# Pairwise field interactions: GpSimd's loads in 8 KB packets, for tiles 4 to 30 instead of 2 to 26

## The chip, the cores and the metric

The kernel runs on one core of one Trainium2 chip. The metric is the device time of one launch in microseconds (us). The kernel before was run six times: median 1326.73 us, lowest 1326.18, highest 1327.6. A smaller time is better.

## What is computed

There are 4096 rows; each has 32 fields of 64 float32 numbers. For each of the 496 pairs of fields (i < j), field i is multiplied by that pair's own 64x64 matrix, and the product is multiplied, element by element, by field j:

```python
i_idx, j_idx = np.triu_indices(32, k=1)
vi = inputs[:, i_idx, :]                       # (4096, 496, 64)
vj = inputs[:, j_idx, :]
vdotw = jnp.einsum('bpd,pde->bpe', vi, W)      # W: (496, 64, 64)
inter = vdotw * vj
return inter.reshape(B, -1)                    # (4096, 31744)
```

The input is 33.6 MB, the matrices 8.4 MB with their padding, and the output 520 MB: the kernel is, before anything else, a writer.

## The kernel before, in words

**Tiles.** The 4096 rows are cut into 32 tiles of 128 rows (row = partition). A tile of x is 128 partitions of 2048 floats, so 8 KB for each partition and 1 MB in all; its output is 128 partitions of 31744 floats, 16.25 MB. All the matrices stay in SBUF in the tile `w`. They come in five pieces on SP's queue (line 194, the list `LOADS`), 928 KB to 2592 KB each.

**Work on one tile.** `transpose_x` (lines 177 to 183) turns x with TensorE, and ScalarE copies the result into `xT`. For each pair p of fields (2p, 2p+1), TensorE multiplies `xT` by the pair's matrices into PSUM (line 222), and VectorE multiplies what is in PSUM by the other fields of x into the SBUF tile `ring` (lines 232 and 240). When the pairs of one of the four groups in `STORES` are done, SP issues that group's store (line 246): 3776, 3264, 3936 and 4896 KB. `ring` has room for 28160 floats a partition, less than one tile's 31744, so VectorE's writes to a part of it wait until the store that last read that part is complete. A store's 128 rows go out on 16 DMA engines, 8 rows on each, every row as one packet of 26112 to 39168 bytes.

**Loads of x.** `xbuf` has three slots of one tile. `x_slots` (line 34) pairs the tiles into loads: tile 0 alone, then (1,2), (4,3), (5,6), (8,7), and so on. The load of tiles t+1 and t+2 stands ahead of tile t's work (lines 200 to 202). A pair none of whose tiles is in `LIGHT_TILES` is one 2 MB DMA from ScalarE's queue (line 157), with 16 KB packets, since the two slots lie side by side. In the other pairs the odd tile is a 1 MB DMA from ScalarE's queue with 8 KB packets, and the even one is issued by GpSimd in `load_beside` (lines 131 to 145). GpSimd's load waits only for its own slot.

**Which DMA engines a GpSimd load uses.** The code assumes a cursor[...]. `from_engine(e)` (lines 119 to 129) moves the cursor to engine e with a tiny DMA, a "nudge" of k rows of 32 bytes. `load_beside` issues four DMAs for a tile:

- a nudge to one of the engines in `PAIRS_FROM`;
- the tail, partitions 120 to 127 (64 KB): 2 engines, 4 rows of 8 KB on each;
- a nudge to engine 5 (`LIGHT + 1`);
- the head, partitions 0 to 119 (960 KB): 15 engines from number 5 round to number 3. Engine `LIGHT` = 4 carries nothing of it. The head is cut into left and right halves of the rows, so that each of the 15 engines gets 16 pieces of 4 KB.

`HEAD` is 120 and `REST` is 4 here. The host lays x out in the order in which the DMAs read it (lines 261 to 276), with 16 floats of padding behind each of the tail's two blocks. GpSimd issues these 52 DMAs in program order and nothing else of weight. Its tiles are 2, 4, ... 26, thirteen of 32.

Of the kernel before, what the change touches and what calls it, by code (L numbers as in the profile page):

```python
# [12 lines left out]
P = 128  # L13
# [10 lines left out]

DMA_ENGINES = 16
LIGHT = 4
LIGHT_TILES = range(2, 28, 2)
PAIRS_FROM = [6, 8, 10, 12, 14, 0, 1]
HEAD = P - P % (DMA_ENGINES - 1)
REST = (P - HEAD) // 2  # L30
PAD = 16


def x_slots(NT):


    loads = [[(0, 0)]]
    for t in range(1, NT, 2):
        if t + 1 == NT:
            loads.append([(t, 1)])  # L40
        elif loads[-1][-1] == (t - 1, 2):
            loads.append([(t + 1, 0), (t, 1)])
        else:
            loads.append([(t, 1), (t + 1, 2)])
    return loads
# [3 lines left out]
def pair_bilinear_kernel(  # L49
# [33 lines left out]
    NT = out.shape[1] * 2 // (F * (F - 1) * D)  # L83
# [16 lines left out]
    def runs(tl, a, b, n):  # L100
# [3 lines left out]

    xbuf = const.tile([P, 3 * F * D], F32, tag="x", name="x")
    x_loads = x_slots(NT)
    x_sizes = [
        sum(P * F * D + (2 * PAD if t in LIGHT_TILES else 0) for t, s in load) for load in x_loads
    ]
    slot = {t: xbuf[:, ts(s, F * D)] for load in x_loads for t, s in load}  # L110

    nudges = [const.tile([DMA_ENGINES, 16], F32, tag=f"nudge{i}", name=f"nudge{i}") for i in range(2)]
    cursor = 0

    def from_pool(out, in_):

        tc.keep_in_program_order(nc.gpsimd.dma_start(out=out, in_=in_))  # L117

    def from_engine(e):

        nonlocal cursor
        k = (e - cursor) % DMA_ENGINES
        if k:
            nudge = nudges[e == LIGHT + 1]
            from_pool(
                nudge[:k].rearrange("p (h c) -> p h c", h=2)[:, :, :4],
                x[: k * 8].rearrange("(p h c) -> p h c", p=k, h=2),
            )
        cursor = e

    def load_beside(at, xt, lap):

        nonlocal cursor
        n = F * D
        from_engine(PAIRS_FROM[lap % len(PAIRS_FROM)])
        g = REST * n + PAD
        tail = x[at + HEAD * n : at + HEAD * n + 2 * g].rearrange("(g c) -> g c", g=2)
        from_pool(xt[HEAD:], tail[:, : REST * n])
        cursor += 2
        from_engine(LIGHT + 1)  # L140
        from_pool(
            xt[:HEAD].rearrange("p (h c) -> p h c", h=2),
            x[at : at + HEAD * n].rearrange("(h p c) -> p h c", h=2, p=HEAD),
        )
        cursor = LIGHT

    def load_x(load):

        at = sum(x_sizes[: x_loads.index(load)])
        parts = [[(t, s)] for t, s in load] if any(t in LIGHT_TILES for t, s in load) else [load]  # L150
        for part in parts:
            t, s = part[0]
            n = len(part) * F * D
            if t in LIGHT_TILES:
                load_beside(at, slot[t], LIGHT_TILES.index(t))
            else:
                nc.scalar.dma_start(
                    out=xbuf[:, s * F * D : s * F * D + n],
                    in_=x[at : at + P * n].rearrange("(p c) -> p c", p=P),
                )  # L160
            at += P * n + (2 * PAD if t in LIGHT_TILES else 0)

    pring = psum.tile([P, BANKS * BANK], F32, tag="pring", name="pring")
    bank = 0
# [21 lines left out]
    at = 0  # L186

    load_x(x_loads[0])
    w_sb = const.tile([P, sum(width[0::2])], F32, tag="w", name="w")
    done = 0  # L190
# [7 lines left out]
    for t in range(NT):  # L198
        xt = slot[t]
        for load in x_loads:  # L200
            if min(load)[0] == t + 1:
                load_x(load)
        for s, group in enumerate(STORES):
            if at + store_w[s] > RING:
                at = 0
# [3 lines left out]
            for p in group:  # L209
# [5 lines left out]
                for c1 in range(first, width[2 * p] + 1, BANK):  # L215
                    n = first if c1 == first else BANK
# [78 lines left out]
```

## Time and profile before

| | before |
|---|---|
| median of six runs | 1326.73 us |
| the profiled execution | 1326.36 us |
| its span, first to last instruction | 1324.2 us |
| mean granted TensorE clock | 0.967 |
| TensorE busy | 1161.5 us (88%) |
| VectorE busy | 1183.2 us (89%) |
| ScalarE busy | 66.1 us (5%) |
| GpSimd busy | 32.5 us (2%) |
| moved by DMA | 562.9 MB, 425 GB/s over the span |

Times on the page are microseconds unless marked ns. The page cuts the span into 40 slices; a digit is the busy share in tenths. A DMA packet is what one DMA engine moves at one go for one queue. The queues are q1 (SP: stores and w), q10 (ScalarE: x), q0 (GpSimd: x and nudges) and two that fetch instructions (q8 and q14). The trace keeps start, duration, queue and size of every packet, but not the number of the DMA engine that moved it.

### The profile page before, as it was taken

Reading aid. Unit: us, or ns where it says so; the run is one execution under the profiler, and the core shown is the slowest. Engines: PE = TensorE matmul, PEld = TensorE weight load, DVE = VectorE, ACT = ScalarE, POOL = GpSimd, SP = SyncE. Lnnn points to the kernel's source line nnn. Section 1 sums busy time; section 2 is a strip of 40 time slices with the busy share of each in tenths; the row PEclk is TensorE's granted clock in tenths of the full one; section 3 lists DMA queues with packets and bytes.
Section 4 is the critical chain, followed back from the end, with each engine's and each line's share of the span. In section 5 each row is a group of like instructions: output and inputs, shape, how many; then the busy total and the mean of one; then the engine's idle time right before and its main releaser. Section 6 shows DMA issues by size and latency. Waiting matters only on the chain.

```text
span 1324.2 us, 13175 instructions
## 1 busy us (share of the span) xinstructions
PE 1161.5 (88%) x5376; PEld 541.1 (41%) x5376; DVE 1183.2 (89%) x1376; ACT 66.1 (5%) x65; POOL 32.5 (2%) x58
## 2 busy tenths in 40 slices
PE   5998989989898998998889889898998979989893
PEld 3443444434343434444344444334444434443441
DVE  4898989989899998998899899898998989989894
ACT  0000000000000000000000000000000000000000
POOL 1000000000000000000000000000000000000000
PEclk9999999999999998999999989999998989989997
DMA  9999999999999999999999999999999999999998
GB/s 336 434 427 433 426 433 430 431 429 425 430 431 429 432 430 428 430 431 433 424 429 426 429 431 426 430 427 434 427 425 432 431 426 434 423 429 432 427 424 358
DMA packets 27068, 562.90 MB, mean 425 GB/s; under 512 B 4584, under 2 KB 4584, under 8 KB 7960
## 3 DMA queue, kind: packets, MB, share of 16 engines
q1 hardware_dynamic: 19152, 528.49, 93.3%
q10 hardware_dynamic: 2448, 19.92, 3.6%
q0 software_dynamic: 5408, 13.65, 2.7%
q8 instruction: 42, 0.69, 0.2%
q14 instruction: 18, 0.15, 0.0%
HBM read 41.95 MB, written 520.09 MB: 424 GB/s over the span
## 4 chain that ended last, share of the span: by engine, by line
DMA 48%; DVE 37%; issue 8%; PE 4%; DVEq 0%; ACT 0%
DMA out_dram<-ring 48%; DVE ring L232 32%; DVE ring L240 5%; PE pring L222 4%; DMA x<-in_x_dram 1%; PE pring L182 0%; DVEq L232 0%; ACT xT L183 0%; DVEq L291 0%; DVEq L240 0%
## 5 line engine op out<-in xcount | busy, mean ns | idle before, releaser
L222 PE MATMUL pring<-w,xT 64*128 64x512 f32 (+4 forms) x4864 | 1097.0, 561 | 133.4 <-DVE ring L232 113.2
L232 DVE TENSOR_TENSOR ring<-pring,x 128x1024 f32<-128x1024 f32 (+3 forms) x1056 | 1104.3, 1107 | 113.2 <-DMA out_dram<-ring 81.2
L222 PEld LDWEIGHTS pring<-w,xT 64*128 64x128 f32 x4864 | 484.1, 190 | 704.4 <-DVE ring L232 524.2
L183 ACT COPY xT<-pring 128x1024 f32<-128x1024 f32 x64 | 64.8, 1012 | 1213.1 <-PE pring L182 1213.1
L240 DVE TENSOR_TENSOR ring<-pring,x 128x64 f32<-128x64 f32 (+3 forms) x320 | 97.5, 355 | 10.0 <-DMA out_dram<-ring 8.9
L182 PEld LDWEIGHTS pring<-ident,x 128*128 128x128 f32 x512 | 57.0, 144 | 59.0 <-DVE ring L232 47.9
L182 PE MATMUL pring<-ident,x 128*128 128x128 f32 x512 | 72.5, 286 | 9.7 <-DMA x<-in_x_dram 9.6
L117 POOL DMA_DIRECT2D x<-in_x_dram x26 | 17.2, 663 | 911.0 <-DVE ring L240 911.0
L117 POOL DMA_DIRECT2D nudge<-in_x_dram x26 | 14.7, 567 | 4.4 <-DMA nudge<-in_x_dram 4.2
L183 ACT ACT_TABLE_LOAD x1 | 1.3, 1283 | 1.7 <-PEq L287 1.7
masks.py:199 POOL TENSOR_SCALAR_AFFINE_SELECT ident<-ident 128x128 f32<-128x128 f32 x1 | 0.3, 287 | 0.1
masks.py:197 POOL MEMSET ident<- 128x128 f32 x1 | 0.2, 205 | 0.3 <-POOLq L287 0.3
L287 POOL MEMSET const-float32-0.0<- 128x1 f32 x1 | 0.1, 93 | 0.2 <-issue 0.2
L287 POOL MEMSET const-bfloat16-1.0<- 128x1 bf16 x1 | 0.1, 95 | 0.0
L287 POOL MEMSET const-uint8-127<- 128x1 uint8 x1 | 0.1, 95 | 0.0
L287 POOL MEMSET const-float32-1.0<- 128x1 f32 x1 | 0.1, 93 | 0.0
## 6 DMA issues: line engine op xcount, KB each, us to landing
out_dram<-ring SPq DMA_DIRECT2D x32, 4896.0 KB, 17.7
out_dram<-ring SPq DMA_DIRECT2D x32, 3936.0 KB, 17.7
out_dram<-ring SPq DMA_DIRECT2D x32, 3776.0 KB, 18.6
out_dram<-ring SPq DMA_DIRECT2D x32, 3264.0 KB, 19.9
x<-in_x_dram ACTq DMA_DIRECT2D x15, 1024.0 KB, 18.9
x<-in_x_dram POOLq DMA_DIRECT2D x13, 960.0 KB, 33.7
x<-in_x_dram ACTq DMA_DIRECT2D x2, 2048.0 KB, 21.6
w<-in_w_dram SPq DMA_DIRECT2D x1, 2592.0 KB, 33.8
```

The costliest lines, as they stand in the source:

```text
L117: tc.keep_in_program_order(nc.gpsimd.dma_start(out=out, in_=in_))
L182: nc.tensor.transpose(pt[:, ts(c, P)], xt[:, ts(n * g + c, P)], ident)
L183: nc.scalar.copy(xT[:, ts(g, 2 * BANK)], pt)
L222: nc.tensor.matmul(pm[:, h * BANK : h * BANK + n], xT[h * D : (h + 1) * D, ts(p, P)], w_sb[h * D : (h + 1) * D, a : a + n], start=True, st ...
L232: nc.vector.tensor_tensor(runs(osb, o[0], o[1], n), runs(pm, 0, BANK, n), bass.AP(xj.tensor, xj.offset, [xj.ap[0], [0, 2], xj.ap[1]]), ALU ...
L240: nc.vector.tensor_tensor(osb[:, o[h] + h * D : o[h] + n], pm[:, h * (BANK + D) : h * BANK + n], xj[:, h * D :], ALU.mult,)
L287: nc = bacc.Bacc("TRN2", target_bir_lowering=False, num_devices=1)
```

## The change

The tiles that GpSimd loads become 4 to 30, even numbers without 16: again thirteen. Tiles 2 and 16 are now in pairs that hold no tile of GpSimd, (1,2) and (16,15), so each of these pairs is one 2 MB DMA on ScalarE's queue. Tiles 28 and 30 leave the 2 MB DMAs of before, and 27 and 29 come as 1 MB DMAs from ScalarE.

In `load_beside` the head is no longer cut into half rows. Both parts are now blocks of whole rows with 16 floats of padding behind each block: 2 blocks of 4 rows for the tail, 15 blocks of 8 rows for the head. The order (nudge, tail, nudge, head), the engines meant and the list `PAIRS_FROM` stay.

```diff
-LIGHT_TILES = range(2, 28, 2)
+LIGHT_TILES = [4, 6, 8, 10, 12, 14, 18, 20, 22, 24, 26, 28, 30]
 PAIRS_FROM = [6, 8, 10, 12, 14, 0, 1]
-HEAD = P - P % (DMA_ENGINES - 1)
-REST = (P - HEAD) // 2
+HEAD = P // DMA_ENGINES
+REST = HEAD // 2
 PAD = 16
...
-        n = F * D
-        from_engine(PAIRS_FROM[lap % len(PAIRS_FROM)])
-        g = REST * n + PAD
-        tail = x[at + HEAD * n : at + HEAD * n + 2 * g].rearrange("(g c) -> g c", g=2)
-        from_pool(xt[HEAD:], tail[:, : REST * n])
-        cursor += 2
-        from_engine(LIGHT + 1)
-        from_pool(
-            xt[:HEAD].rearrange("p (h c) -> p h c", h=2),
-            x[at : at + HEAD * n].rearrange("(h p c) -> p h c", h=2, p=HEAD),
-        )
-        cursor = LIGHT
+        most = DMA_ENGINES - 1
+        for e, k, rows, p in (
+            (PAIRS_FROM[lap % len(PAIRS_FROM)], 2, REST, most * HEAD),
+            (LIGHT + 1, most, HEAD, 0),
+        ):
+            from_engine(e)
+            n = rows * F * D
+            blocks = x[at : at + k * (n + PAD)].rearrange("(k c) -> k c", k=k)
+            from_pool(xt[p : p + k * rows], blocks[:, :n])
+            at += k * (n + PAD)
+            cursor = (e + k) % DMA_ENGINES
```

The rest of the diff gives x the new sizes and lays it out on the host to match.

More of the change, by code (lines that the diff above doesn't have):

```diff
@@ L106, in pair_bilinear_kernel @@
     x_loads = x_slots(NT)
-    x_sizes = [
-        sum(P * F * D + (2 * PAD if t in LIGHT_TILES else 0) for t, s in load) for load in x_loads
-    ]
+    pads = (DMA_ENGINES + 1) * PAD
+    tile_sizes = [P * F * D + (pads if t in LIGHT_TILES else 0) for t in range(NT)]
+    x_sizes = [sum(tile_sizes[t] for t, s in load) for load in x_loads]
     slot = {t: xbuf[:, ts(s, F * D)] for load in x_loads for t, s in load}
@@ L160, in load_x @@
                 )
-            at += P * n + (2 * PAD if t in LIGHT_TILES else 0)
+            at += sum(tile_sizes[t] for t, s in part)
     pring = psum.tile([P, BANKS * BANK], F32, tag="pring", name="pring")
@@ L269 @@
             if t in LIGHT_TILES:
-                x.append(rows[:HEAD, t].reshape(HEAD, 2, -1).transpose(1, 0, 2).ravel())
-                tail = np.zeros((2, REST * F * D + PAD), rows.dtype)
-                tail[:, : REST * F * D] = rows[HEAD:, t].reshape(2, -1)
-                x.append(tail.ravel())
+                k = (DMA_ENGINES - 1) * HEAD
+                for part in (
+                    rows[k:, t].reshape(2, REST * F * D),
+                    rows[:k, t].reshape(DMA_ENGINES - 1, HEAD * F * D),
+                ):
+                    x.append(np.pad(part, ((0, 0), (0, PAD))).ravel())
             else:
```

## The prediction

> **What bounds the kernel now.** I read the 40 slices first, then busy time by stage, the DMA queues, the DMA issues, and last the packets themselves.
>
> ```profile
> DVE  4898989989899998998899899898998989989894
> ...
> DMA  9999999999999999999999999999999999999998
> GB/s 336 434 427 433 426 433 430 431 429 425 430 431 429 432 430 428 430 431 433 424 429 426 429 431 426 430 427 434 427 425 432 431 426 434 423 429 432 427 424 358
> ```
>
> The DMA engines are full in every slice; VectorE, the next, has gaps throughout. So the end is set by the bytes and by the pace of the 16 DMA engines. Two slices are below some 425 GB/s: the first and the last. By stage:
>
> ```profile
> 2.00:8.00 6.00, 0.00 (x0) 0.00 (x0) 0.00 (x0) 0.95 (x1) 2.13 (x4) 1.00 0.93 371
> 8.00:27.00 19.00, 12.87 (x54) 6.80 (x56) 10.30 (x10) 1.01 (x1) 0.60 (x1) 1.00 1.03 326
> 27.00:34.00 7.00, 7.00 (x40) 5.07 (x38) 6.58 (x8) 1.01 (x1) 0.00 (x0) 1.00 0.99 424
> ...
> 60.00:1300.00 1240.00, 1114.62 (x5166) 516.08 (x5163) 1137.37 (x1320) 61.73 (x61) 26.75 (x45) 0.97 1.00 429
> 1300.00:1324.20 24.20, 3.67 (x22) 1.84 (x19) 6.30 (x12) 0.00 (x0) 0.00 (x0) 0.63 0.76 328
> ```
>
> The last two numbers of a line are DMA share and GB/s. From 8 to 27 us the engines are fully busy and yet move only 326 GB/s: packets take longer there. In the last stretch they are 76% busy: some engines have finished while others run on. These two are what the change can touch.
>
> ```profile
> q1 hardware_dynamic: 19152, 528.49, 93.3%
> q10 hardware_dynamic: 2448, 19.92, 3.6%
> q0 software_dynamic: 5408, 13.65, 2.7%
> ...
> x<-in_x_dram ACTq DMA_DIRECT2D x15, 1024.0 KB, 18.9
> x<-in_x_dram POOLq DMA_DIRECT2D x13, 960.0 KB, 33.7
> x<-in_x_dram ACTq DMA_DIRECT2D x2, 2048.0 KB, 21.6
> ```
>
> q0 takes 0.198% of the engines' time per MB (2.7/13.65), q10 0.181%.
>
> **The packets.** On one engine a packet starts 3 to 4 ns before the one ahead of it ends, so the records can be joined into 16 chains, one for each engine (identities can swap where two engines coincide). Four readings:
>
> - Usual durations: 159 ns for 4096 bytes, 309 for 8192, 611 for 16384; a store's row 968 (26112 bytes) to 1448 (39168).
> - In the slow stage a w packet of 7424 bytes takes 370 ns (281 alone), 13312 bytes 706 (some 497 at the rate of the rest), 16128 bytes 758 (601 alone), x of 8192 bytes 410, x of 4096 bytes 205. The excess of all loads after 8.1 us is 79.4 us, 4.96 us an engine. It begins with w's second piece beside tile 1 (q10), goes on beside tile 2 (q0), and is gone within a microsecond of tile 2's last packet at 26.7: w alone runs at 601 and 771 ns (20736 bytes). The stores' first rows start at 34.4 us on the median engine, 32.4 on the first.
> - One engine is slow throughout: 33 ns more than usual on the median store row from 980 us on; its excess is 8.5 us there, the others' 0.4 to 2.8. It is the one that carries none of GpSimd's heads. Until tile 26's head (959 to 980 us) it stays within about 1.5 us of the median engine; from 1003 to 1306 us it falls from 1.27 ahead to 4.60 behind, 0.8 us a tile. It ends at 1322.70, the next at 1321.96, the median at 1318.9.
> - During a head the slow engine gets 16 empty packets of 4 bytes in place of 16 pieces. In seven heads its packets took 1.10 to 2.27 us over the usual, of which 22 x 33 ns = 0.73 is its own slowness: 23 to 96 ns an empty packet, mean 62.
>
> [...] 15 chains get pieces, one gets none. [...] GpSimd's head, 16 packets an engine, lands after 33.7 us, ScalarE's load, 8 packets, after 18.9. [...] here 2 x 159 - 309 = 9 ns. [...]
>
> **The change part by part.**
>
> *8 KB packets.* 120 pairs of 4 KB become 120 packets of 8 KB in 13 tiles: 120 x 13 x 9 ns = 14.0 us, over 15 engines 0.9 us each. It lies on the bound. The tails keep their form. Loads land sooner, which nobody waits for.
>
> *Empty packets.* Tails of 4 rows give 4 empty packets on each other engine (728 = 13 x 14 x 4 in q0's count), so a head of 8 rows should give 8 instead of 16. Of the 12 later heads, 96 empty packets fewer: 96 x 62 ns = 6.0 us on the slow engine; ends 2.2 and 9.2. Nothing excludes that one costs more when it is rarer; I take zero as the outer bound.
>
> *Which tiles.* The slow engine is spared thirteen heads before and after. Tiles 28 and 30 spare it at about 1040 and 1120 us, where it falls behind now; tile 2's relief (2.0 us in the first store's start) and tile 16's are lost. Its total stays; only the empty packets make it shorter. Because it has no gaps of its own, its end moves with its total.
>
> *The start.* Tile 2 leaves q0. Up to 7.3 us (w's first piece and tile 0 at usual durations) nothing changes. Then 8 rounds of 281 ns (w) and 611 ns (tiles 1 and 2) make 7.14 us. The unknown is whether they slow each other. Below: not at all, as w's first piece beside tile 0. Above: w stays slow for all of its middle pieces. I take the ratio of w beside tile 1, 370/281 and 410/309, 1.33: 9.5 us, to 16.8. Then w alone: 8 x 497 = 4.0, 8 x 601 = 4.8, 8 x 771 = 6.2: 31.8 us in place of 34.4, **2.6 us** saved. VectorE covers this: the first store is issued at 23.93 us, long before; tile 0's last store is issued at 57.87 while the engines have rows until 61.95, 4 us of cover. Without the slowing, 29.4 us, 5.0 saved, and perhaps 0.3 lost because that cover is used up. The slow engine carries tile 2 now and is 2% slower: 32.4, no gain there.
>
> *What is moved past whom.* On ScalarE one DMA replaces a tile's; it is 5% busy. Tiles 15 and 16 wait for the later slot and land in 21.6 us instead of 18.9; tile 1's start at 57.75 and the turning of tile 2 at 85.44 show 27.7 us until the data is needed, so 6 us of cover remain. If that were gone, TensorE would wait once. On GpSimd the first tail, tile 4's, waits for tile 0's end as now:
>
> ```profile
> 8.31 0.60 POOL L117 DMA_DIRECT2D nudge<-in_x_dram  x1 [4.17 <-DMA nudge<-in_x_dram]
> 58.14 0.57 POOL L117 DMA_DIRECT2D x<-in_x_dram  x1 [49.23 <-DVE ring L240]
> ```
>
> Behind it are only its own loads, needed tens of us later. SP's queue is untouched.
>
> *Sum.* Slow engine: 1322.70 - 6.0 = 1316.7. The next engine: 1321.96 - 2.6 - 0.9 = 1318.5, which is then last. That is 4.2 us before 1322.70. The profiled execution took 1326.36 (span 1324.2 and 2.2 around it), so 1322.1; the median of the runs is 0.4 higher: **1322.5**.
>
> **Rivals.**
>
> *No slowing left at the start* (25%). For it: w's first piece and tile 0 are both at usual durations, and most of the slow stage has q0 in it. Against: w and tile 1 slow each other from 8.2 us, three before q0's first 4 KB piece at 11.24. 5.0 - 0.3 in place of 2.6: 1320.4.
>
> *The slow engine stays last* (17%). Empty packets cost the same whatever their number, or are still 16. Its total is then as before: 1322.7 less 2.2 to 0, so 1324.5 to 1326.7.
>
> *Slower* (7%). w's middle pieces stay slow to the end although tile 2 has left q0, and the slow engine has tile 2 on top: 7.3 + 1.35 x 1.02 x (2.25 + 4.9 + 4.0 + 4.8) + 6.3 = 35.6 us in place of 32.4. With no help from empty packets: +3.2, 1329.9. It decides from where the slow engine's first store row starts later than 32.4 by more than the empty packets give back.
>
> *The change doesn't do what it says* (3%). [...] The tails, of the same form, go to two engines today.
>
> **Numbers.** Likeliest 48%, 1322.5 (own range 1321 to 1324.3). The range 1319.8 to 1326.3 leaves out the slower cases and the edges. About 0.2%, 2.65 us, is what a measurement can tell from no change, so faster is under 1324.1: the likeliest case, the first rival and a little of the second, 0.75; same 0.16; slower 0.09.
>
> **What would show it.** Right: no 4096-byte packets in q0; the stage from 8 to 27 us well above 326 GB/s, first store rows near 31.8; 104 empty head packets in place of 208; the slow engine no longer last. Wrong: w still at 700 ns after tile 2's last packet, or one engine still 3 us behind the median at the end.

## The result and the profile after

The kernel after takes 1322.74 us (median of 18 runs, 1320.04 to 1325.33); the kernel before, run again beside it, 1326.41 (38 runs). The ratio is 0.9971, 95% interval 0.9965 to 0.9977: 3.7 us or 0.3% faster, where 1322.5 had been forecast. The profiled execution of the kernel after took 1323.68 us, with a span of 1321.5.

First the same two rows of slices, and q0, of the kernel after:

```profile
DMA  9999999999999999999999999999999999999998
GB/s 392 434 429 431 429 427 426 434 433 420 427 428 412 440 421 429 430 429 431 428 429 428 430 434 424 430 425 426 423 433 426 425 428 424 424 431 430 428 434 377
...
q0 software_dynamic: 3744, 13.65, 2.5%
```

The first slice rose from 336 to 392 GB/s and the last from 358 to 377; in between some slices are lower than before (412, 420, 421). q0 moves the same 13.65 MB in 3744 packets instead of 5408: 1560 fewer x packets, and 104 fewer empty ones, as counted ahead. By stage:

```profile
2.00:8.00 6.00, 0.00 (x0) 0.00 (x0) 0.00 (x0) 0.94 (x1) 0.27 (x1) 1.00 0.95 381
8.00:27.00 19.00, 16.71 (x68) 8.21 (x70) 12.08 (x12) 2.02 (x2) 0.00 (x0) 1.00 1.01 430
27.00:34.00 7.00, 7.00 (x36) 2.92 (x32) 7.00 (x8) 0.00 (x0) 0.00 (x0) 1.00 1.03 412
...
60.00:1300.00 1240.00, 1113.78 (x5152) 516.36 (x5154) 1135.78 (x1318) 61.74 (x61) 26.50 (x47) 0.98 1.00 428
1300.00:1321.50 21.50, 2.09 (x14) 0.98 (x10) 4.05 (x10) 0.00 (x0) 0.00 (x0) 0.59 0.81 350
```

From 8 to 27 us the engines now move 430 GB/s, not 326: the slow stage is gone entirely, not in part. The long middle is a little slower, 428 in place of 429 (428.02 and 429.22 before rounding), which over 1240 us is some 3 us. The loads of GpSimd do land sooner (26.3 us in place of 33.7), and nobody was waiting for them:

```profile
x<-in_x_dram ACTq DMA_DIRECT2D x15, 1024.0 KB, 18.7
x<-in_x_dram POOLq DMA_DIRECT2D x13, 960.0 KB, 26.3
x<-in_x_dram ACTq DMA_DIRECT2D x2, 2048.0 KB, 18.2
```

In the packet records of the kernel after each head still lies on 15 of the 16 chains, 8 packets of 8192 bytes on each, and the sixteenth gets 8 empty ones. ScalarE's 1 MB loads of 128 partitions put 8 packets on each of 16 chains, in both kernels. That the new head would stay on 15 engines was not shown before the run, and which numbers the engines of the code have in the chip, no trace shows.

The packet records give an account, in us for the mean of the 16 engines. They are of one execution each (1326.36 and 1323.68 us), and packet times are without the 3.5 ns by which a packet overlaps the next. "Excess" is what a packet took over the usual duration of its size; idle time is counted from 35 to 1310 us.

```
                                     before    after
w, packet time                        23.66    20.65
x from ScalarE, packet time           47.37    46.69
x from GpSimd, packet time            33.21    31.99
stores, packet time                 1207.08  1209.09
  of it excess                         7.21     9.22
idle                                   1.85     2.90
first store row, median engine         34.4     30.1
last store row ends, mean engine    1319.45  1317.90
last store row ends, last engine    1322.70  1320.03
```

The start gives 4.4 us, and only 2.7 arrive at the end of these two executions. Two things ate into it that the prediction did not have: the stores' rows got longer by 2.0 us an engine, and the engines stood idle for 1.05 us more.

### The profile page after: what moved, and what is told of

Same layout as the page of the kernel before. It is cut to its first block, busy times and chain, and to the rows that moved or that the text cites. A ratio compares the mean times of both kernels' runs of the same rounds, so it can differ in the third digit from the quotient of the medians.

```text
span 1321.5 us, 13176 instructions
## 1 busy us (share of the span) xinstructions
PE 1163.7 (88%) x5376; PEld 539.4 (41%) x5376; DVE 1183.5 (90%) x1376; ACT 66.1 (5%) x65; POOL 30.2 (2%) x58
## 3 DMA queue, kind: packets, MB, share of 16 engines
q0 software_dynamic: 3744, 13.65, 2.5%
## 4 chain that ended last, share of the span: by engine, by line
DMA 48%; DVE 35%; issue 8%; PE 7%; DVEq 0%; ACT 0%
DMA out_dram<-ring 47%; DVE ring L231 31%; PE pring L221 6%; DVE ring L239 4%; DMA x<-in_x_dram 1%; PE pring L181 0%; DVEq L231 0%; ACT xT L182 0%; DVEq L292 0%; DVEq L239 0%
## 5 line engine op out<-in xcount | busy, mean ns | idle before, releaser
L231 DVE TENSOR_TENSOR ring<-pring,x 128x1024 f32<-128x1024 f32 (+3 forms) x1056 | 1104.4, 1107 | 106.2 <-DMA out_dram<-ring 71.5
## 6 DMA issues: line engine op xcount, KB each, us to landing
x<-in_x_dram POOLq DMA_DIRECT2D x13, 960.0 KB, 26.3
```

What stands on the lines that cost most here:

```text
L231: nc.vector.tensor_tensor(runs(osb, o[0], o[1], n), runs(pm, 0, BANK, n), bass.AP(xj.tensor, xj.offset, [xj.ap[0], [0, 2], xj.ap[1]]), ALU ...
```

## Experiments

Each was compared with the kernel before on the same chip (1326.05 to 1326.52 us there). They ran on three chips, so kernels that are compared with each other are best compared by these ratios. The diffs leave out what lays x out on the host, and some of them the lines that set `apart` and `parts` as the first diff on the start does.

### Each part alone

Tile 2 from ScalarE, nothing else (before):

```diff
-LIGHT_TILES = range(2, 28, 2)
+LIGHT_TILES = range(4, 28, 2)
```

> One part alone: the kernel before, but tile 2 comes with tile 1 in one 2 MB DMA from ScalarE (GpSimd's tiles 4 to 26, twelve of them, still in 4 KB pieces). Theory: w's second to fourth piece read at full speed once nothing of GpSimd's is in flight beside them, and the ordinary engines reach the first store near 30 us instead of 34.4. The slow engine, which now carries tile 2 too, gains only some 2.4 us and has no help after 980 us, so it ends last: 1324 us. Rival (the gain is made at the end, by the heads of tiles 28 and 30): no gain here, 1326.4 or more.

Measured: 1321.10 us, ratio 0.9961 (0.9949 to 0.9974). By stage it already has the start of the kernel after:

```profile
8.00:27.00 19.00, 16.75 (x72) 8.15 (x74) 12.82 (x14) 2.02 (x2) 0.00 (x0) 1.00 1.01 432
```

So the start alone is worth 5.4 us, twice the 2.4 expected. In the records the slow engine is still last, 3.76 us behind the median engine's end, as before; but the median itself moved from 1318.9 to 1313.4, and the slow engine with it, from 1322.7 to 1317.2.

The 8 KB pieces alone (the kernel after with the tiles of before):

```diff
-LIGHT_TILES = [4, 6, 8, 10, 12, 14, 18, 20, 22, 24, 26, 28, 30]
+LIGHT_TILES = range(2, 28, 2)
```

> One part alone: the kernel after, but with the list of tiles of before (2 to 26), so only the 8 KB pieces are new. Theory: the start stays slow (w near 700 ns a packet beside tile 2), 8 KB pieces give the ordinary engines 0.5 to 0.9 us, and the slow engine some 0.2 us a head through fewer empty packets; if 8 KB pieces lengthen the stores' rows, 2 us go back. 1325 to 1326.5. Rival (8 KB pieces are what gains): 1322.7.

Measured: 1327.86 us, ratio 1.0011 (1.0003 to 1.0019): the 8 KB pieces alone are a small loss. The start is as slow as ever, or a little slower (first store rows at 35.0 us, 34.4 before):

```profile
8.00:27.00 19.00, 11.13 (x46) 6.16 (x47) 8.71 (x8) 1.01 (x1) 0.58 (x1) 0.97 1.02 309
```

The profiled execution took 1326.40 us, the shortest of the thirteen, and its stores' excess is 7.47 us an engine, hardly more than before (7.21). So the trace does not show the whole of the loss that the median shows.

The new list of tiles alone, heads in 4 KB pieces (before):

```diff
-LIGHT_TILES = range(2, 28, 2)
+LIGHT_TILES = [4, 6, 8, 10, 12, 14, 18, 20, 22, 24, 26, 28, 30]
```

> The other part alone: the kernel before with the new list of tiles, heads still in 4 KB pieces. Theory: nearly the whole gain, 1322.5 to 1324. If it is the 8 KB pieces that lengthened the store rows by 2.0 us an engine, rows here have the excess of before (7.2 us an engine, not 9.2) and the time is at or below 1322.7. Rival (8 KB pieces are what gains): 1326.

Measured: 1319.15 us, ratio 0.9947 (0.9933 to 0.9960). That is better than the whole change. Its slices:

```profile
DMA  9999999999999999999999999999999999999998
GB/s 393 432 434 430 427 433 431 430 431 426 429 428 434 430 425 429 429 432 431 432 429 426 431 436 415 437 422 428 430 428 431 428 430 426 432 429 433 427 431 378
DMA packets 27068, 562.90 MB, mean 427 GB/s; under 512 B 4584, under 2 KB 4584, under 8 KB 7960
```

The first slice is that of the kernel after (393), and the dips to 420 and 412 in slices 10 and 13 are not there (the lowest here is 415, in slice 25). The stores' excess is 6.63 us an engine, the idle time 0.60. Against the kernel with tile 2 alone the median engine ends at the same 1313.4, but the last one at 1315.56 instead of 1317.19: that is what the heads of tiles 28 and 30 do, about 2 us in the medians (1321.10 to 1319.15; the two intervals overlap).

No heads at all (the kernel after with an empty list):

```diff
+LIGHT_TILES = []
```

> GpSimd loads nothing: all of x comes from ScalarE, in 2 MB DMAs, so all 16 engines carry the same. Theory: the slow engine loses some 1.6 us of relief for each of thirteen tiles and holds up the ring for all: 1326.4 + 13 x 1.6 - 2.4 = 1345 us; its rows are at full duration plus 33 ns and all others wait. Rival (empty packets and nudges cost as much as the relief gives): 1326 or below.

Measured: 1337.02 us, ratio 1.0080 (1.0068 to 1.0093). That is 17.9 us above the list alone (1337.02 - 1319.15), 1.4 us for each of thirteen heads. The engines stand idle 14.3 us on average, and VectorE waits 95.8 us for stores before its multiplications (71.5 in the kernel after), which fits waiting for the slow one. But not all of it is relief lost: with the list empty, nearly all loads are 2 MB with 16 KB packets, and the stores' excess is 11.36 us an engine, not 6.63. Of this 6.4 us lie in the rows that an engine was moving when the first 16 KB packet of such a load came up; two thirds of them took 0.61 to 0.63 us longer, just the time of that packet. How the 17.9 us divide between the two was not measured. The expectation, 1345, had too small a gain at the start and 1.6 us a head.

### What slowed w at the start

Tiles 1 and 2 as two DMAs from ScalarE (kernel after):

```diff
-        parts = [[(t, s)] for t, s in load] if any(t in LIGHT_TILES for t, s in load) else [load]
+        apart = any(t in LIGHT_TILES or t == 2 for t, s in load)
+        parts = [[(t, s)] for t, s in load] if apart else [load]
```

> The kernel after, with tiles 1 and 2 as two 1 MB DMAs from ScalarE (8 KB packets) instead of one of 2 MB (16 KB packets). What freed the start: if it is that nothing of GpSimd's is in flight there, w stays at 281 and 498 ns a packet and the time at 1322.7; if it is the 16 KB packets or the merged DMA, w goes back to 370 beside tile 1 and to some 700 beside tile 2, and the time to 1326.

Measured: 1321.93 us, ratio 0.9971 (0.9960 to 0.9981), w at 281 and 498 ns:

```profile
8.00:27.00 19.00, 16.95 (x72) 8.29 (x74) 12.99 (x14) 2.02 (x2) 0.00 (x0) 1.00 1.02 434
```

Neither the 16 KB packets nor the merging matter for the start: 434 GB/s without them, 430 with them.

Tile 2 from GpSimd, as one plain load of 128 partitions (on top of the new list, 4 KB pieces):

```diff
+            elif t == 2:
+                from_pool(slot[t], x[at : at + P * n].rearrange("(p c) -> p c", p=P))
```

> The new list with heads in 4 KB pieces (1319.15 us), but tile 2 comes from GpSimd again at the start, as one plain DMA of 128 partitions on all 16 engines, without tail, nudges or empty packets. If a transfer of GpSimd's beside w is what slows w, w is near 700 ns beside tile 2 and the time near 1323; if it is [...] the empty packets, w stays at 498 and the time at 1319.

Measured: 1318.46 us, ratio 0.9939 (0.9926 to 0.9951), w at 281 and 498 ns:

```profile
8.00:27.00 19.00, 15.60 (x68) 7.90 (x70) 11.75 (x12) 1.81 (x2) 0.00 (x0) 1.00 1.02 434
```

So it is not GpSimd's queue, nor three queues at once: 434 GB/s with tile 2 on it.

Tile 2 from ScalarE, 120 partitions and then 8 partitions:

```diff
+            elif t == 2:
+                for a, b in ((0, HEAD), (HEAD, P)):
+                    nc.scalar.dma_start(
+                        out=slot[t][a:b],
+                        in_=x[at + a * n : at + b * n].rearrange("(p c) -> p c", p=b - a),
+                    )
```

> The new list with heads in 4 KB pieces (1319.15 us), but tile 2 comes from ScalarE in two DMAs, 120 partitions on 15 engines and 8 partitions: the head's spread without GpSimd, nudges or empty packets. If the spread itself [...] is what slows w, w's 13312-byte packets are near 700 ns beside it and the time near 1323; if GpSimd's nudges, tail or empty packets are the cause, w stays at 498 and the time at 1319.

Measured: 1322.22 us, ratio 0.9968 (0.9957 to 0.9978), 3.1 us above the list alone, though the two ratios' intervals just overlap (0.9933 to 0.9960 there). In the profiled execution (1325.78 us, the longest of eight) the start is slow again, with first store rows at 35.2 us, not 30.1:

```profile
8.00:27.00 19.00, 13.92 (x48) 7.23 (x50) 9.45 (x9) 1.01 (x1) 0.00 (x0) 0.93 1.02 307
```

307 GB/s, with no load of GpSimd's in these 19 us. w's 13312-byte packets take 802 ns on the mean and its 16128-byte ones 792 (601 alone), while its second piece, beside tile 1, keeps 281. So it is the form of the load, 120 partitions and 8 in place of 128, that slows the other load, whoever issues it.

Tile 2's 120 partitions from GpSimd, without a nudge:

```diff
+            elif t == 2:
+                nc.scalar.dma_start(
+                    out=slot[t][HEAD:],
+                    in_=x[at + HEAD * n : at + P * n].rearrange("(p c) -> p c", p=P - HEAD),
+                )
+                from_pool(slot[t][:HEAD], x[at : at + HEAD * n].rearrange("(p c) -> p c", p=HEAD))
+                cursor = DMA_ENGINES - 1
```

> As the one before, but tile 2's 120 partitions come from GpSimd on 15 engines in 8 KB packets, without a nudge, and the 8 partitions from ScalarE, so only the head's own eight empty packets are left. If the spread over 15 engines is the cause, w is near 700 ns as in the kernel before; if tail and nudges are, w stays at 498.

Measured: 1345.79 us, ratio 1.0149 (1.0135 to 1.0162). At the start it agrees:

```profile
8.00:27.00 19.00, 12.21 (x48) 6.39 (x50) 8.95 (x9) 1.01 (x1) 0.00 (x0) 1.00 1.02 306
```

w's second piece takes 441 ns and its third 637 on the mean. The third is slow once more in a stretch of its own: from 20.0 us, when GpSimd's load is over and only the 8 partitions from ScalarE are left beside w, one packet on each of eight engines, w's 13312-byte packets take up to 1598 ns. So a spread over 8 engines slowed w too; the slowing isn't tied to 15.

The time tells of something else. The edit sets `cursor` to 15 after this DMA, and in the records of the later heads one engine gets no pieces and another, the slow one, gets its 16: the relief goes to a wrong engine. It ends 27 us above the list alone, of which some 5.8 us are the slow start (first store rows at 35.95 us, 30.1 there).

### What the 8 KB pieces cost

More padding, so that all reads start at multiples of 512 bytes in x (kernel after):

```diff
-PAD = 16
+PAD = 128
```

> The kernel after with 128 floats of padding behind each block instead of 16, so every block and every load of x starts at a multiple of 512 bytes. If 8 KB pieces cost 3.6 us because the 64-byte shift of each block makes the reads uneven, the rows' excess falls from 9.2 to near 6.6 us an engine and the time to 1319 to 1320; if it is the length of the pieces, nothing changes: 1322.7.

Measured: 1321.81 us, ratio 0.9968 (0.9955 to 0.9980), excess 8.81 us an engine. It stays with the other kernels of 8 KB pieces; the shift of the blocks is not the cause, or not most of it.

Pieces of 2 KB (new list):

```diff
-            xt[:HEAD].rearrange("p (h c) -> p h c", h=2),
-            x[at : at + HEAD * n].rearrange("(h p c) -> p h c", h=2, p=HEAD),
+            xt[:HEAD].rearrange("p (h c) -> p h c", h=4),
+            x[at : at + HEAD * n].rearrange("(h p c) -> p h c", h=4, p=HEAD),
```

> The new list with heads in pieces of 2 KB (32 an engine) instead of 4 KB. If longer pieces lengthen the store rows during heads (2.9 to 3.5 us an engine in 8 KB, 2.0 in 4 KB), rows have less excess with 2 KB, under 1.6 us; against that stand [...] 32 empty packets a head on the slow engine: 1319 to 1321. If the number of empty packets is what matters, with a fixed cost each, the slow engine loses 16 x 60 ns a head more, 12 us, and the time is above 1325.

Measured: 1319.82 us, ratio 0.9951 (0.9938 to 0.9965). The records show no 2048-byte packets: 3120 of 4096 bytes, as with 4 KB pieces, and the empty ones joined in pairs as well (8 bytes). So this isn't the third point of a series: the same packets gave the same time (1319.82 us, and 1319.15 for the list alone).

Tails from ScalarE (new list, 4 KB pieces):

```diff
-        from_engine(PAIRS_FROM[lap % len(PAIRS_FROM)])
...
-        from_pool(xt[HEAD:], tail[:, : REST * n])
-        cursor += 2
+        for i in range(2):
+            nc.scalar.dma_start(
+                out=xt[HEAD + i * REST : HEAD + (i + 1) * REST],
+                in_=tail[i, : REST * n].rearrange("(p c) -> p c", p=REST),
+            )
```

> The new list with heads in 4 KB pieces, and the tails of all thirteen tiles from ScalarE [...] instead of GpSimd: 728 of the 936 empty packets and half of the nudges go. If an empty packet costs the packet behind it some 26 ns on average (24 us over 936 in the kernel before), 1.2 us an engine are saved: 1318. Rival: [...] 1325 or more.

Measured: 1338.11 us, ratio 1.0091 (1.0077 to 1.0104). It doesn't answer its question: the nudges of one engine that the edit makes went out as two packets of 16 bytes each (24 of them for twelve nudges), and in the records the slow engine gets its 16 pieces during most heads: its relief is gone in those. The time is near that of no heads at all (1337.02). What an empty packet of a tail costs was not measured.

Tile 16 with a head as well (new list, fourteen heads of 4 KB pieces):

```diff
+LIGHT_TILES = range(4, 32, 2)
```

> The new list with tile 16 as well (fourteen heads, 4 KB pieces). If the slow engine is still what ends last in the list of thirteen, one more head spares it 1.6 us and the time falls to 1318; if it no longer is, the others carry one head more (0.17 us each) and nothing changes: 1319.2.

Measured: 1318.74 us, ratio 0.9944 (0.9932 to 0.9957). Nothing clear of the spread is gained over thirteen.

## Why the prediction was right in the sum and wrong in its steps

**The bound: right.** The 16 DMA engines are full (9 tenths or more) in all slices but the last (8 tenths) of the kernels before and after and of the list alone, and changes in packet time and in balance are what moved the end.

**The start: right mechanism, mis-sized term, and the wrong reading of the cause.** The prediction let w and tiles 1 and 2 go on slowing each other by 1.33 and came to 2.6 us. The first rival was right instead: no slowing left, 430 GB/s, first rows at 30.1 in place of 34.4, and 5.4 us in the end when this part is made alone. What spoke against the rival was that w slowed from 8.2 us, three us before GpSimd's first 4 KB piece at 11.24. But the tail's eight packets, a spread over two engines, were in flight from 7.3 to 10.3 us, and the w packets that start in the half microsecond from 11.0 are back within 7% of their usual time before the head slows them again. The cause that the experiments single out is the form of the load: 120 partitions, and 8 on eight engines, slowed w beside them by ScalarE's queue too (802 ns on the mean and up to 1598), and 128 didn't even by GpSimd's (498). Why such a load does this, no run shows. Beside stores such heads do far less: 0.57 to 2.34 us a head, 16 engines together, in either line of the table in the next step; the excess of the loads at the start was 79.4 us.

**8 KB pieces: the sign was wrong.** The step had them save 0.9 us an engine. By the records they do save, though less, since successive packets overlap by 3.5 ns: 5.5 ns a pair, not 9, and 0.5 us an engine. But in the time they cost 1.4 us alone and 3.6 on top of the list (1322.74 against 1319.15, different runs, the ratios' intervals apart). The rows of the stores that are under way when a head begins get longer:

```
excess of the store rows, 16 engines together, us a head (mean over the heads after 50 us)
                                            4 KB packets    8 KB packets
                                            (7 kernels)     (4 kernels)
rows that end 0 to 4 us after its start     0.57 to 0.86    1.63 to 2.34
rows that end 4 to 24 us after it           1.72 to 2.29    2.02 to 2.13
```

In the first line all seven kernels are on one side and all four on the other; in the second they are not apart. (Left out are the two kernels with 4 KB heads whose relief went astray, where rows are longer throughout.) Over thirteen heads the first line makes 1.0 us an engine between the list alone (0.62) and the kernel after (1.62). The rest is in rows elsewhere (1.6), which the 8 KB pieces with the old list don't show, and in 2.3 us more idle time; for these no run gives the cause. Nor is it a matter of the 15 engines or of GpSimd: the row that an engine is on when a load's first packet comes up is often longer by up to about that packet's time, ScalarE's loads on 16 engines included. With ScalarE's 16 KB packets (611 ns) 0.61 to 0.63 us were usual in the kernel without heads; ahead of a head, the longest tenth began at 0.30 to 0.35 us with 8 KB packets and at 0.10 to 0.16 with 4 KB. Why this is so stays open. It is not, in the main, where the reads start (1321.81 us with all of them at multiples of 512 bytes in x).

**Empty packets: right in number, wrong in price.** There are 104 fewer, as forecast. The prediction priced each at 62 ns whatever its rarity, 6.0 us on the slow engine, and kept zero as outer bound. A head costs the slow engine as much as ever: its rows that overlap a head have an excess of 1.1 us in the kernel after, 1.0 in the list alone, 1.2 before. In its rows, runs of some 200 to 330 ns follow one another where those of 4 KB heads had some 110 to 190. Half as many packets, twice the price. So the second rival was right in this, though not in its time: the slow engine is still last, at 1320.03 and not 1316.7, 2.5 us behind the median. That is short of the 3 us named as a sign of being wrong, but the slow engine no longer last, named as a sign of being right, didn't come. It matters little for the time: an ordinary engine ends at 1319.9, only 0.1 us earlier, where the prediction had 1318.5 for the last of these, so 6 us given back on the slow engine would by themselves have moved the end by 0.1 us.

**Which tiles: understated.** "Its total stays", the prediction said of the slow engine, with no gain at the start. With tile 2 alone taken away it ended 5.5 us earlier than before, one head fewer notwithstanding, and still 3.76 us behind the median. With the new list it ends at 1315.1, another 2.1 us earlier, while the median stays; an ordinary engine is then the last, at 1315.56. The list of thirteen has the heads of tiles 28 and 30 more than that kernel, and that of tile 16 less.

**The sum.** Forecast: -2.6 and -0.9 on the engine that would be last, about -3.9 on the median. Found: -5.4 (start) - 2.0 (late heads) + 3.6 (8 KB pieces) = -3.8. Two terms were too small by 2.8 and 2.0 and one had the wrong sign and was off by 4.5; they cancel. These are steps from one kernel to the next, so they add up by themselves; in another order they have other sizes (the 8 KB pieces cost 1.4 us with the old list), and the intervals of the kernel with tile 2 alone and of the list alone overlap. The forecast of 1322.5 is right to 0.2 us by luck.

**What was moved past whom: right.** VectorE's cover at the start held: VectorE is done with tile 0 at 53.1 us instead of 57.8, and the stage from 34 to 60 us runs at 431 GB/s. ScalarE's larger loads kept no engine waiting (TensorE waits for x only once, for tile 0: 8.9 us, 9.6 before), and GpSimd's first wait costs nothing:

```profile
1.58 0.69 POOL L117 DMA_DIRECT2D nudge<-in_x_dram  x1 [0.27 <-issue]
53.51 0.59 POOL L117 DMA_DIRECT2D x<-in_x_dram  x1 [51.24 <-DVE ring L239]
```

**A better version.** Heads in 4 KB pieces with the new list, and tile 2 either from ScalarE (0.9947) or plainly from GpSimd (0.9939): their intervals overlap, and both are below the kernel after's.

## What to carry to other kernels

Where the DMA engines are the bound, ask of each transfer which engines it runs on and what loads beside it, not only how many bytes and packets it has: here a load of 120 partitions beside another load brought the rate of all down from some 430 to some 310 GB/s, while the same bytes in a load of 128 left it at 430 to 434; beside stores such heads cost little (0.57 to 2.34 us a head, 16 engines together, in either line of the table). Make each part of a change alone before believing a sum that fits: here three wrong terms added up to the right time. Take no price per packet from one packet size to another without a run: here half as many empty packets cost the slow engine as much as before (1.1 us a head, 1.0 to 1.2 with twice as many), and heads in 8 KB packets made the store rows that end within 4 us of a head's start longer than heads in 4 KB did (1.63 to 2.34 us a head, 0.57 to 0.86).

## What the runs showed that was not expected

- A load of 120 partitions and one of 8 beside w: 307 GB/s (both from ScalarE) and 306 (the 120 from GpSimd, 8 KB packets), against 430 to 434 with loads of 128.
- The slow engine is as slow when GpSimd issues no DMA at all: some 20 to 42 ns over the usual on its median row in most of the last stores of the kernel without heads.
- With the start at full rate, w's last piece takes 834 to 876 ns a packet on the mean in place of 771, with packets of over 1000 ns beside the first store rows; no run was made to find out why.
- Pieces of 2 KB travelled as packets of 4096 bytes (3120 of them, none of 2048), 8 KB rows as packets of 8192.
- Heads that spare a wrong engine gave nothing back: 1345.79 us against 1337.02, of which some 5.8 us are the slow start of that kernel.
